# A two-layer graph kernel: the edge stage of each layer written out in source order, with its sums, node work and table writes cut into small steps

## The chip, the cores and the metric

The kernel runs on one core of a Trainium2 chip. The metric is the device time of one execution in microseconds (us). Engines are named as in the profile: PE (TensorE), DVE (VectorE), ACT (ScalarE), POOL (GpSimd) and SP (SyncE); PE, DVE, ACT and POOL compute, and SP, ACT and POOL also issue DMA transfers.

## What is computed

Two graph-transformer layers over 6250 nodes and 100,000 edges with 8 heads of 16 channels, then a linear layer, a residual and a layer norm. The edges are sorted by their target `dst`. Cut to what matters here:

```python
def gt_layer(x, ntype, etype, src, dst, Wk, Wq, Wv, Wa, Watt, Wmsg, pri, skip, g, b):
    k = typed_linear(x, ntype, Wk).reshape(n, H, HS)
    q = typed_linear(x, ntype, Wq).reshape(n, H, HS)
    v = typed_linear(x, ntype, Wv).reshape(n, H, HS)
    kT = jnp.einsum('nhd,htdo->nhto', k, Watt)
    vT = jnp.einsum('nhd,htdo->nhto', v, Wmsg)
    kw = kT[src, :, etype]
    m = vT[src, :, etype]
    a = jnp.einsum('ehd,ehd->eh', kw, q[dst]) * pri[:, etype].T / SQRT_D
    att = edge_softmax(a, dst, n)
    msg = (m * att[:, :, None]).reshape(-1, H * HS)
    hag = jax.ops.segment_sum(msg, dst, num_segments=n)
    h = jax.nn.silu(typed_linear(hag, ntype, Wa))
    alpha = jax.nn.sigmoid(skip[ntype])[:, None]
    h = h * alpha + x * (1.0 - alpha)
    ...
    return (h - mu) * jax.lax.rsqrt(var + 1e-05) * g + b
```

`typed_linear` uses one of 16 weight matrices for each node, by its type. So kT and vT together are a table with one row of 256 numbers for every pair of a node and one of 32 edge types, and each edge takes one row of it.

## The kernel before

**Tables.** For each layer the table is a DRAM tensor of 200,704 rows of 1 KB (`tabs`). The table of layer 0 is written first, from the inputs, beside the counting and ranking of nodes. The table of layer 1 is written by the node work of layer 0.

**Blocks.** The nodes are ranked into 52 blocks of 128, one node to a partition: 4 classes of 4 node types each, 13 blocks a class, by falling number of edges. A block has as many *slots* as its deepest node can have edges: 40, 23, 21, 19, 18, 17, 17, 16, 15, 14, 13, 12 and 11 in each class, 236 a class and 944 a layer. `superblocks` groups the 13 blocks of a class as 3, 3, 3 and 4, 16 superblocks in all.

**Edge work** (`edges`, from L737). For each slot POOL issues one indirect DMA (L754), which gathers 128 table rows, one for each partition, into a quarter of a `kv` tile. A `kv` tile holds a *chunk* of 4 slots (`CH`), and there are 12 of them. For each chunk DVE multiplies keys and query (L766) and adds up over the channels (L768). When a block's chunks are through, DVE adds the mask, takes the maximum and subtracts it (L773 to L778), ACT takes the exponential (L780), and DVE weighs the values of each chunk (L790), adds them into `acc` (L795) and reduces them (L796). Only L790 and L795 release a `kv` tile.

**Node work** (`nodes`, from L841). For each superblock: transpose on PE (L215), typed linear with `xm` masks on DVE (L200, PE L209), tanh on ACT (L856), residual (L865), norm statistics (L838, L839), reciprocal root by 13 small DVE instructions (`rstd_of`, L819 to L832), and norm (L872, L874). In layer 0 three typed linears follow, and then `table_block` (L220): for each block two halves of the edge types, each with 8 PE products of 32 rows (L229) and 8 ACT copies from PSUM into an `st` tile of 2 MB (L236), which POOL scatters into the table of layer 1 with one indirect DMA (L891). In layer 1 the last linear layer follows, and POOL scatters each block's output with one indirect DMA (L922). So POOL issues 944 gathers and 104 table scatters in layer 0, and 944 gathers and 52 output scatters in layer 1.

**What orders the work.** `edges` calls a generator `beside` once a chunk; it yields the queries of the next superblock and then the node work of the superblock before. This is the order in the source only. The program's scheduler, which works by priorities, is free to place the instructions of each engine otherwise, within the dependences; on each engine they then run in the order that it chose. The first gather of layer 1 depends on all table scatters (`puts`). Consecutive output scatters write the same tensor, and each waits for the one before to be complete; each POOL DMA also waits for the one eight places before it. PSUM pools: `qwp` 2 buffers, `accp` 2, `nps` 4, which the node work and `table_block` share under the name `nb`.

Of the kernel before, what the change touches and what calls it, by code (L numbers as in the profile page):

```python
# [9 lines left out]
F32 = mybir.dt.float32  # L10
# [3 lines left out]
ALU = mybir.AluOpType  # L14
# [55 lines left out]
def kernel(  # L70
# [91 lines left out]
    def load_edge_weights(l):  # L162
# [8 lines left out]

        nc.vector.tensor_scalar(prit, prit, 1.0 / float(HS) ** 0.5, None, op0=ALU.mult)
# [5 lines left out]
    load_edge_weights(0)  # L178
    load_typed(wq0, Wq[0])
# [38 lines left out]
    def table_block(pool, ps_pool, kT, vT, i, share, bufs, store):  # L218


        for tg in range(TG):
            tt = slice(tg * 16, (tg + 1) * 16)
            st = pool.tile([P, 16, 2 * D], F32, name="st", bufs=bufs)
            for half, (yT, bd) in enumerate(((kT, bdk), (vT, bdv))):
                for hp in range(HP):
                    s = slice(hp * 2 * HS, (hp + 1) * 2 * HS)
                    pt = ps_pool.tile([P, SB * P], F32, name="nb").rearrange(
# [450 lines left out]
    def arm(fast):  # L678

        puts = []  # L680
        ep = ctx2.enter_context(tc.tile_pool(name="ep", bufs=2))
        npl = ctx2.enter_context(tc.tile_pool(name="npl", bufs=1))
        qwp = ctx2.enter_context(tc.tile_pool(name="qwp", bufs=2, space=PSUM))
        accp = ctx2.enter_context(tc.tile_pool(name="accp", bufs=2, space=PSUM))
        nps = ctx2.enter_context(tc.tile_pool(name="nps", bufs=4, space=PSUM))
# [3 lines left out]
        if fast:  # L689
            for c in range(NC):  # L690
                for i0, k in superblocks(CB):
                    sbs.append((c * CB + i0, k, range(c * TC, (c + 1) * TC)))
        else:
            sbs = [(i0, k, range(TY)) for i0, k in superblocks(NB)]
# [9 lines left out]
        def old_rows(of, i0, k):  # L704
            hr = npl.tile([P, SB, D], F32, name="hr", bufs=3)
            nc.sync.dma_start(hr[:, :k], rows(of, i0, k))
            return hr

        def q_rows(ps, k):

            qT = npl.tile([P, SB * P], F32, name="qT")
# [3 lines left out]
            q = ep.tile([P, SB, D], F32, name="q")  # L715
# [3 lines left out]
        def queries0(got, i0, k, types):  # L719
# [6 lines left out]
            q = yield from q_rows(ps, k)  # L726
            got.append((q, ntb, hr))

        def queries1(got, i0, k, types):
            q = ep.tile([P, SB, D], F32, name="q")  # L730
            nc.sync.dma_start(q[:, :k], rows(qrd[1], i0, k))
            got.append((q, types_of(i0, k), old_rows(hrd, i0, k)))
            yield

        def edges(l, i0, k, q, beside):


            sums = ep.tile([P, SB, D], F32, name="sums")
            den = ep.tile([P, SB, H], F32, name="den")
            for i in range(k):  # L740
                b = i0 + i
                K = KB[b]
                qw = qwp.tile([P, 512], F32, name="qw")
                nc.scalar.copy(qw[:, :D], q[:, i, :])
                a = ep.tile([P, max(KB), H], F32, name="a")
                w = qw[:, D:D + K * H].rearrange("p (k h) -> p k h", h=H)
                chunks = [(j, min(j + CH, K)) for j in range(0, K, CH)]
                kvt = []
                for j0, j1 in chunks:
                    kv = ep.tile([P, CH, 2 * D], F32, name="kv", bufs=12)  # L750
                    kvt.append(kv)
                    for j in range(j0, j1):
                        at = KO[b] + j
                        get = nc.gpsimd.indirect_dma_start(  # L754
                            out=kv[:, j - j0, :], out_offset=None, in_=tabs[l][:],
                            in_offset=bass.IndirectOffsetOnAxis(ap=ell[:, at:at + 1], axis=0))
                        if l == 1:
                            for put in puts:
                                tc.add_manual_dep(
                                    get.ins, put.ins.name,  # L760
                                    mybir.DependencyInfo(mybir.DependencyClass.Sync,
                                                         mybir.DependencyReason.DATA),
                                    reason="rows of the table")
                            puts.clear()
# [33 lines left out]
            for _ in beside:  # L798
                pass
# [274 lines left out]
```

## Time and profile before

| | us |
|---|---|
| median of 3 runs (3934.1 to 3941.8) | 3939.6 |
| profiled execution, its own time | 3934.5 |
| its span in the trace | 3932.6 |
| first gather of layer 0's edge stage | at 918.3 |
| last gather of layer 0 | at 2420.3 |
| first gather of layer 1 | at 2589.1 |
| last gather of layer 1 done, about | at 3873.4 |
| DVE busy in the span | 2144.5 (55%) |
| POOL busy in the span | 2057.5 (52%) |
| PE busy in the span | 1969.3 (50%) |
| ACT busy in the span | 922.7 (23%) |

The page gives the busy time of each engine, the span in 40 slices, the costliest groups of instructions with the idle time ahead of them and what ended it. The trace can be asked for stretches of time, for waits by engine and for a timeline. `L754` is line 754 of the kernel before. `<-issue` after an idle time says that nothing which the profile shows ended it.

### The profile page before, as it was taken

The page shows a single profiled execution, that of the slowest core. Times are in us where ns is not written, and L with a number is a line of the kernel's source. Part 1 is how long each engine was busy: PE and PEld are TensorE (multiplying, and loading weights), DVE is VectorE, ACT ScalarE, POOL GpSimd, SP SyncE. Part 2 cuts the span into 40 slices and gives each one's busy share as a digit, 9 for nine tenths or more (in the row PEclk, how much of TensorE's full clock was granted, in tenths as well). Part 3 has the DMA queues.
Part 4 walks back from the last instruction along what each step waited for, and adds up shares of the span by engine and source line. Part 5 has one row for each costly group of instructions (what it writes and reads, how often), then busy time and mean ns, then how long its engine had stood idle before and what let it go on. Part 6 is the DMA issues. An engine that isn't in the chain of part 4 may idle for free. (4 is left out here: it accounts for less than half of the span.)

```text
span 3932.6 us, 25934 instructions
## 1 busy us (share of the span) xinstructions
PE 1969.3 (50%) x6850; PEld 1039.2 (26%) x6850; DVE 2144.5 (55%) x4929; ACT 922.7 (23%) x1928; POOL 2057.5 (52%) x2157
## 2 busy tenths in 40 slices
PE   2899967993165555666566657820221221122022
PEld 1345523331033333333234334410110110011011
DVE  6975632433655555455545554126655665665565
ACT  0244323451033232333233224420000000000000
POOL 0000072004766667656665664057776776777773
PEclk9999977995565566666666666755555555555555
DMA  4367548787366554675466558543343443333331
GB/s 89 160 264 310 239 132 324 324 339 248 104 215 218 199 205 162 244 262 207 146 241 259 199 176 306 204 159 115 110 113 95 115 112 102 109 111 107 105 103 51
DMA packets 216823, 716.14 MB, mean 182 GB/s; under 512 B 64437, under 2 KB 122670, under 8 KB 191615
## 3 DMA queue, kind: packets, MB, share of 16 engines
q0 software_dynamic: 110592, 459.50, 35.5%
q1 hardware_dynamic: 83425, 245.01, 16.2%
q10 hardware_dynamic: 22642, 9.82, 1.1%
q8 instruction: 58, 0.95, 0.1%
q14 instruction: 106, 0.87, 0.1%
HBM read 289.27 MB, written 438.40 MB: 185 GB/s over the span
## 5 line engine op out<-in xcount | busy, mean ns | idle before, releaser
L754 POOL DMA_INDIRECT kv<-tab,ell x1888 | 1795.4, 951 | 928.8 <-issue 504.4
L236 ACT COPY st<-nb 128x512 f32<-128x512 f32 x1420 | 738.3, 596 | 661.9 <-PE nb L229 428.0
L766 DVE TENSOR_TENSOR kv<-kv,qw 128x512 f32<-128x512 f32 (+3 forms) x512 | 326.7, 642 | 923.7 <-DMA kv<-tab,ell 890.7
L229 PE MATMUL nb<-bdv,kvT 32*128 32x512 f32 x832 | 385.3, 1042 | 144.9 <-ACT st L236 144.4
L229 PE MATMUL nb<-bdk,kvT 32*128 32x512 f32 x832 | 364.1, 1013 | 122.7 <-ACT st L236 122.7
L644 PE MATMUL l<-xm,wkqv 128*128 128x512 f32 (+1 forms) x832 | 395.4, 608 | 8.1 <-DVE xm L200 8.1
L215 PE MATMUL nb<-ident,hag 128*128 128x128 f32 x104 | 24.5, 366 | 597.2 <-DVE hag L809 597.2
L768 DVE TENSOR_REDUCE a<-kv 128x32 f32<-128x512 f32 (+3 forms) x512 | 320.6, 636 | 0.9
L566 POOL DMA_INDIRECT ell<-kvs,start x52 | 53.9, 1037 | 504.5 <-DVE gap L545 489.0
L200 DVE SCALAR_TENSOR_TENSOR xm<-ntb,nb 128x384 f32<-128x384 int32 (+1 forms) x256 | 133.2, 582 | 310.0 <-PE nb L215 310.0
L215 PE MATMUL nb<-ident,hs 128*128 128x128 f32 x104 | 32.6, 456 | 520.0 <-DVE hs L874 481.8
L891 POOL DMA_INDIRECT tab<-st,row x104 | 104.5, 1005 | 336.4 <-ACT st L236 322.3
L780 ACT ACTIVATE qw<-a 128x136 f32<-128x136 f32 (+11 forms) x104 | 30.7, 296 | 1002.7 <-DVE a L778 984.9
L795 DVE TENSOR_TENSOR acc<-kv,acc 128x512 f32<-128x512 f32 (+3 forms) x408 | 259.0, 635 | 0.2
L229 PEld LDWEIGHTS nb<-bdv,kvT 32*128 32x128 f32 x832 | 188.6, 282 | 266.0 <-ACT st L236 265.0
L234 DVE COPY st<-nb 128x512 f32<-128x512 f32 x196 | 135.1, 689 | 211.3 <-PE nb L229 113.4
L790 DVE TENSOR_TENSOR kv<-kv,qw 128x512 f32<-128x512 f32 (+3 forms) x408 | 247.4, 626 | 0.0
L229 PEld LDWEIGHTS nb<-bdk,kvT 32*128 32x128 f32 x832 | 173.5, 274 | 216.6 <-ACT st L236 207.0
L644 PEld LDWEIGHTS l<-xm,wkqv 128*128 128x128 f32 x832 | 149.4, 195 | 237.6 <-issue 207.2
L229 PE MATMUL nb<-bdv,yT 32*128 32x512 f32 x784 | 171.1, 695 | 65.5 <-ACT st L236 62.7
L200 DVE SCALAR_TENSOR_TENSOR xm<-ntb,hT 128x512 f32<-128x512 int32 (+1 forms) x208 | 133.9, 658 | 114.8 <-PE l L644 105.2
L209 PE MATMUL nb<-xm,wkqv 128*128 128x384 f32 (+1 forms) x384 | 173.7, 619 | 20.2 <-DVE xm L200 20.2
(197 smaller groups left out, 2339.9 us busy)
## 6 DMA issues: line engine op xcount, KB each, us to landing
tab<-st SPq DMA_DIRECT2D x98, 2048.0 KB, 7.1
kv<-tab,ell POOLq DMA_INDIRECT x1888
ntb<-typed SPq DMA_DIRECT2D x24, 192.0 KB, 3.2
xrd<-xr SPq DMA_DIRECT2D x13, 256.0 KB, 2.3
hr<-in_x_dram SPq DMA_DIRECT2D x10, 256.0 KB, 4.1
ntb<-in_node_type_dram SPq DMA_DIRECT2D x10, 256.0 KB, 6.7
hr<-xrd SPq DMA_DIRECT2D x12, 192.0 KB, 2.7
hrd<-hs SPq DMA_DIRECT2D x12, 192.0 KB, 2.4
```

Of the source, the lines that this page charges most:

```text
L200: nc.vector.scalar_tensor_tensor(xm[:, :n], ntb[:, :n], float(t), hT[:, :n], op0=ALU.is_equal, op1=ALU.mult)
L209: nc.tensor.matmul(ps[:, :n], w[:, t, :], xm[:, :n], start=(t == types[0]), stop=(t == types[-1]))
L229: nc.tensor.matmul(pt, yT[s, i * P:(i + 1) * P], bd[s, tt, :], start=True, stop=True)
L234: nc.vector.tensor_copy(to, pt)
L236: nc.scalar.copy(to, pt)
L644: nc.tensor.matmul(ps[i][:, :n], wkqv[:, i, t, :], xm[:, :n], start=(t == 0), stop=(t == TY - 1))
L754: get = nc.gpsimd.indirect_dma_start(out=kv[:, j - j0, :], out_offset=None, in_=tabs[l][:], in_offset=bass.IndirectOffsetOnAxis(ap=ell[:, ...
L766: nc.vector.tensor_tensor(kk, kk, qw[:, :D].unsqueeze(1).to_broadcast([P, j1 - j0, D]), op=ALU.mult)
L768: nc.vector.tensor_reduce(a[:, j0:j1, :], kk.rearrange("p k (h d) -> p k h d", h=H), axis=AX.X, op=ALU.add)
L790: nc.vector.tensor_tensor(to.rearrange("p k (h d) -> p k h d", h=H), v.rearrange("p k (h d) -> p k h d", h=H), w[:, j0:j1, :].unsqueeze(3) ...
L795: nc.vector.tensor_tensor(acc[:, :c], v, acc[:, :c], op=ALU.add)
L891: put = nc.gpsimd.indirect_dma_start(out=tabs[1].rearrange("(n t) c -> n (t c)", t=16), out_offset=bass.IndirectOffsetOnAxis(ap=row2[:, tg ...
```

## The change

- The arm of the program that runs here is recorded under `manual_schedule`: each engine takes its instructions in source order.
- The superblocks of a class are 4, 3, 3 and 3 blocks, with 103, 52, 45 and 36 slots (before: 84, 54, 48 and 50).
- `edges` now goes over a whole layer. The sums of a block (`finished`: mask, maximum, exponential, weighing and adding) are a generator, of which a step is taken after each product, each reduction and once more for each chunk of the *next* block: 3 steps a chunk. The first tile of a block is released in step 5.
- The node work has many more yields (34 steps are reckoned for layer 0 and 50 for layer 1) and is spread over the next superblock's slots.
- The table pieces of a superblock are a second list, spread over the slots of the superblock two further on (faster for the last four). A scatter is emitted three further steps after its tile was handed over, not at once. The last superblock's copies from PSUM are shared by ACT and DVE.
- The output scatters of a superblock are emitted together, 8 yields after the data; those of the last superblock at once.
- PSUM: `accp` 1 buffer, `nps` 2, and `table_block` has its own pool `tps` of 3. `hr` is loaded again for the node work. The scaling of layer 1's edge weights moves into the first node work.

No instruction of the edge work is added or removed: POOL still issues 1048 DMAs in layer 0 and 996 in layer 1. In the built program's POOL order, 13 table scatters follow the last gather of layer 0 (20 before), and the output scatters stand in 14 groups of 3 or 4 ahead of layer 1's last gather, with the last 6 behind it.

```diff
     def arm(fast):
...
-        accp = ctx2.enter_context(tc.tile_pool(name="accp", bufs=2, space=PSUM))
-        nps = ctx2.enter_context(tc.tile_pool(name="nps", bufs=4, space=PSUM))
+            accp = ctx2.enter_context(tc.tile_pool(name="accp", bufs=1, space=PSUM))
+        nps = ctx2.enter_context(tc.tile_pool(name="nps", bufs=2 if fast else 5, space=PSUM))
+        tps = ctx2.enter_context(tc.tile_pool(name="tps", bufs=3, space=PSUM))
...
-                    sbs.append((c * CB + i0, k, range(c * TC, (c + 1) * TC)))
+                    sbs.append((c * CB + CB - i0 - k, k, range(c * TC, (c + 1) * TC)))
+            sbs.sort(key=lambda sb: sb[0])
...
+            def spread(work, gen, steps, slots):
+
+                work.append([gen, steps / slots, 0.0])
+
+            def tick(n):
+                for of in (work, pieces):
+                    if of:
+                        w = of[0]
+                        w[2] += w[1] * n
+                        while w[2] >= 1.0:
+                            w[2] -= 1.0
+                            if next(w[0], of) is of:
+                                of.pop(0)
+                                break
...
+            def finished(s, i, chunks, kvt, a, w, sums, den):
...
+                yield
                 m = ep.tile([P, H], F32, name="m")
                 nc.vector.tensor_reduce(m, av.rearrange("p k h -> p h k"), axis=AX.X, op=ALU.max)
+                yield
                 nc.vector.tensor_tensor(av, av, m.unsqueeze(1).to_broadcast([P, K, H]),
                                         op=ALU.subtract)
                 nc.scalar.activation(w, av, AF.Exp)
-                next(beside, None)
+                yield
+                yield
                 nc.vector.tensor_reduce(den[:, i, :], w.rearrange("p k h -> p h k"),
                                         axis=AX.X, op=ALU.add)
                 acc = accp.tile([P, CH, D], F32, name="acc")
...
+                for j in range(len(chunks) + 1):
+                    if j < len(chunks):
+                        j0, j1 = chunks[j]
+                        v = kvt[j][:, :j1 - j0, D:]
+                        nc.vector.tensor_tensor(
...
+                    if j > 1:
+                        j0, j1 = chunks[j - 1]
+                        nc.vector.tensor_tensor(acc[:, :j1 - j0], kvt[j - 1][:, :j1 - j0, D:],
+                                                acc[:, :j1 - j0], op=ALU.add)
+                    yield
                 nc.vector.tensor_reduce(sums[:, i, :], acc.rearrange("p k c -> p c k"),
                                         axis=AX.X, op=ALU.add)
...
+                if i == k - 1:
+                    spread(work, nodes(l, *sbs[s], sums, den, got[s][1], lambda gen: table(s, gen)),
+                           50 if l else 34, pace(s + 1))
...
+                    tables[s] = gen
+                    spread(pieces, gen, 8 * sbs[s][1] + 4, (1.0 if s + 4 < len(sbs) else 0.6) * slots(min(s + 2, len(sbs) - 1)))
...
+                        nc.vector.tensor_tensor(
+                            kk, kk, qw[:, :D].unsqueeze(1).to_broadcast([P, c, D]), op=ALU.mult)
+                        step()
+                        tick(c / 3)
+                        nc.vector.tensor_reduce(a[:, j0:j1, :],
+                                                kk.rearrange("p k (h d) -> p k h d", h=H),
+                                                axis=AX.X, op=ALU.add)
+                        step()
+                        tick(c / 3)
+                        step()
+                        tick(c / 3)
...
+            while work or pieces:
+                for of in (work, pieces, pieces, pieces):
+                    if of and next(of[0][0], of) is of:
+                        of.pop(0)
...
+            for _ in range(8):
+                yield
+            for i in range(0 if final else k):
+                put_out(o, i0, i)
...
+            def steps(gen):
+
+                for _ in gen:
+                    for _ in range(2):
+                        for what in late:
+                            what[0] -= 1
+                        while late and late[0][0] <= 0:
+                            scatter(*late.pop(0)[1])
+                        yield
+
+            for i in range(k):
+                def store(tg, st, b=i0 + i):
+                    late.append([3, (tg, st, b)])
...
     with tc.If(full < 1) as cmp:
         with ExitStack() as ctx2:
+            ctx2.enter_context(tc.manual_schedule())
             arm(True)
```

## The prediction

> **What bounds the kernel now.** I read the page's busy shares first, then stretches of time by stage, then POOL's timeline and waits. No engine is busy over 55% of the span. The stretches below are the four classes of layer 0, the time between the layers, two classes of layer 1 and the end (columns: stretch, length, busy us and instruction count of PE, PE's weight loads, DVE, ACT and POOL, then clock, DMA share and GB/s):
>
> ```profile
> PE 1969.3 (50%) x6850; PEld 1039.2 (26%) x6850; DVE 2144.5 (55%) x4929; ACT 922.7 (23%) x1928; POOL 2057.5 (52%) x2157
> ```
>
> ```profile
> 918.30:1244.60 326.30, 120.84 (x298) 64.24 (x298) 179.15 (x390) 56.95 (x126) 231.57 (x244) 0.58 0.51 153
> 1244.60:1630.00 385.40, 233.75 (x617) 133.19 (x617) 204.87 (x482) 122.00 (x257) 249.96 (x262) 0.62 0.63 220
> 2025.10:2428.40 403.30, 247.75 (x679) 142.18 (x678) 214.30 (x505) 137.02 (x289) 251.90 (x263) 0.63 0.63 222
> 2428.40:2589.10 160.70, 133.01 (x377) 78.74 (x374) 28.79 (x96) 84.37 (x165) 18.66 (x20) 0.66 0.61 247
> 2895.30:3221.30 326.00, 62.20 (x149) 35.89 (x149) 201.57 (x549) 15.59 (x47) 237.37 (x249) 0.52 0.38 108
> 3873.40:3932.60 59.20, 17.14 (x44) 9.93 (x44) 27.68 (x96) 1.43 (x3) 6.92 (x7) 0.56 0.06 16
> ```
>
> POOL's timeline (start, length, idle before) gives the unit: a gather every 1.25 us, 0.95 of work and 0.30 that nothing ends. In layer 1, 249 x 1.25 = 311 of the 326 us. So POOL's issue is the bound there, and a full "busy" POOL shows 76%.
>
> ```profile
> 3609.65 0.95 POOL L754 DMA_INDIRECT kv<-tab,ell  x1 [0.30 <-issue]
> 3610.90 1.25 POOL L754 DMA_INDIRECT kv<-tab,ell  x1 [0.30 <-issue]
> 3619.38 0.94 POOL L754 DMA_INDIRECT kv<-tab,ell  x1 [7.23 <-DVE acc L790]
> 3620.63 0.94 POOL L754 DMA_INDIRECT kv<-tab,ell  x1 [0.30 <-issue]
> ```
>
> The 7.23 us recur once a class: the 40-slot block fills 10 of 12 kv tiles. Other stalls are table scatters that wait for ACT (POOL's waits from 1000 to 2400 us: total, times, longest), and output scatters that follow each other:
>
> ```profile
> POOL tab L891 <- ACT st L236: 178.5, 50, 8.4
> ```
>
> ```profile
> 3917.76 0.98 POOL L922 DMA_INDIRECT out_dram<-o,node  x1 [32.13 <-DVE o L920]
> 3920.76 0.98 POOL L922 DMA_INDIRECT out_dram<-o,node  x1 [2.02 <-issue]
> ```
>
> The ledger, in 1.25 us issues: start 918.3; layer 0, 1048 x 1.25 = 1310, and idle 1670.8 - 1310 = 361; layer 1 up to 3873.4, (944 + 45) x 1.25 = 1236, and idle 48; end 59. Sum 3932.6. Of the 361, the stretch from the last gather's end (2421.3) to layer 1's first (2589.1) holds 168 - 20 x 1.25 = 143, and the steady part 218.
>
> **What the Trainium skill says.** "PSUM — Partial Sum Buffer", section "Engine vs sequencer instructions": ACT, DVE and POOL queues are strict FIFO. So source order is run order, and one late operand holds all behind it; the stalls above agree. "DMA: Bandwidth & Descriptors", section "Anatomy of one DMA — SWDGE (gpsimd) path": a POOL DMA has about 2 us of fixed cost, mostly the receipt. The trace agrees: 2.02 us idle between chained output scatters, which start 3.00 us apart. "Perfetto Trace Analysis", section "Optimization Strategy": look at the gaps of the engine that should be full; a gap that repeats can mean too few buffers. That is the 7.23.
>
> **The change, part by part.**
>
> *POOL's issue work* is unchanged: 1310 in layer 0. In layer 1, 46 output scatters stand ahead of the last gather: 990 x 1.25 = 1237.5. The start (918.3) ends with the table of layer 0, which is not touched; the moved weight scaling is 0.42 + 1.22 us of DVE under POOL's first 48 gathers (60 us), and costs 1.6 us at most without that cover.
>
> *Sums as steps.* No DVE instruction goes. After the 40-slot block only two tiles are free, and its first is released in step 5 of the next block, in that block's second chunk. In layer 1: 1.5 us from issue to landing (from POOL's end to the transfer's semaphore, median of the trace), then product, reduction, sum and weighing (0.69 + 0.68 + 0.49 + 0.68) and a node row or two, about 5 us of stall; the next chunk's gathers take 5 us and its tile comes two DVE steps after landing, 4 us more. 9 us against 7.23, four times a layer: 36. Bounds 24 and 56.
>
> *Table scatters, layer 0 steady.* Before, six scatters came in a cluster one or two gathers apart, which is 3 us of POOL against 5.49 us a tile in ACT and PE (timeline of the tail: 2578.30, then 2583.79). Now they mostly have 4 or more gathers between them (6.25 us), and four half-steps after the last copy. So the rate stall goes. What is late next is position: POOL runs ahead of ACT, and ACT is tied to DVE and PE by exponentials and node work. Where a table tile is pressed into the 45 and 36 slots, the slack is about 5 slots, 7 us, against landing (2.4 on average in layer 0) and a half tile (2.7) with its copies (2.4): 7.5. DMA is at its limit there too: 0.79 x 5.49 = 4.3 us of all queues for a scatter, 4 x 0.39 x 1.25 = 2.0 for its gathers, 6.3 against 6.25. Every later gather queues behind a waiting scatter, and DVE waits for those. No row shows this wait. Bounds: 0, and 218/84 = 2.6 us a scatter as now. I take 0.9 for 91 scatters, 79 us. With 36 for the tile stalls: 115 (was 218).
>
> *Between the layers.* From the last gather's end (T): sums done T+12 (landing, last products, about 15 DVE rows). The tanh stands behind 32 copies in ACT's order, 4 x 5.49 = 22, so T+25. Tanh to key copies took 17.7 before (2458.66 to 2476.34), so T+43; to the first scatter 7.6, T+51; five more at 5.49, T+78; layer 1's gather 5.3 later (2583.79 to 2589.06), T+84. Less 13 x 1.25 = 16: 68, I take 70 (was 143: two chains one after the other). Bounds 62 and 95: the node chain alone takes 37 (2508.1 to 2545.3), or all 48 copies lie ahead of it.
>
> *Output scatters.* A chained one costs 3.00 - 1.25 = 1.75. 14 groups make 46 - 14 = 32 of them: 56. With 36 for tiles and 13 for scatters that wait for DVE in short superblocks (bounds 0 and 40): 105 (was 48). This part loses 57.
>
> *The end.* Before: 13.8 from the last gather to the transposes (3887.16), 30.6 to the first scatter, 3 x 3.0, 5.8 to the end. Now three scatters instead of four and three blocks (2.6 less a block in the last products, 1 to 2 of statistics out of the way): 52 (was 59).
>
> Reloading `hr` is 16 loads on SP's queue, 2.7 us each, behind nothing that gates a gather: nothing, or 3 us at each superblock's transposes if SP were late. PSUM with fewer buffers is inside the 0.9.
>
> Sum: 918.3 + 1310 + 115 + 70 + 1237.5 + 105 + 52 = 3808 span. The profiled execution's own time is 1.9 above its span, and the median 5 above that: **3815 us**, 3.2% less. Main case's own range 3765 to 3900.
>
> **The rivals.**
>
> *Clean*: no scatter waits. 36 + 62 + 92 + 50 in place of 115, 70, 105 and 52 is 102 less: 3713. For it: landing is 1.5 to 2.4 us. Against: the DMA count above.
>
> *The wait only moves*: each scatter still stalls 2.6 us: 91 x 2.6 + 36 = 273 of steady idle for 115, 158 more: 3973. For it: POOL in fixed order runs behind ACT as before. Against: the clusters are gone. No gain is left from 1.4 above my 0.9 a scatter (125 us).
>
> *Slower: DVE in fixed order pays the hand-overs.* Each superblock's node chain has some five places where DVE's next instruction needs PE or ACT. Bare, the tail shows 4.70 us for the tanh and 0.6 to 1.2 for each transpose, about 8 a superblock; behind a table half of 2.7 on PE each, up to 22. In the 45 and 36 slots POOL has (81 + 14) x 1.25 = 119 us. DVE has 0.75 us of edge work a slot (the four kv and acc rows of the groups, 1154 us in both layers, and 1.9 + 0.68 for each of 104 blocks: 1420/1888), 61, and 134/16 = 8.4 of node work and queries a superblock (834 busy in layer 0 less 944 x 0.75 = 708, some 130): 78, so 41 free. Waits of 2 x 8 fit, 2 x 22 just don't; it decides from 20 a superblock (4 a hand-over). If they reach 50, since PE itself waits for ACT's copies, 59 are over in each class, and kv tiles run out: 236 more, 4051. Against: DVE is 53% busy in layer 0, and free kv tiles let POOL run on. For it: the scheduler could place ready work there, source order can't.
>
> **How the numbers follow.** Main 0.58, clean 0.20, wait moves 0.12, hand-overs 0.10. A measurement of this kernel can tell about 0.2% from no change. Faster: main and clean less 0.02 for main's upper end: 0.76; same 0.04; slower, the last two less what falls between: 0.20. The range for 8 in 10 goes from the clean case (3715) to the moving wait (3975).
>
> **What would show it.** Right: POOL's 1.25 us cadence unchanged; layer 0's steady idle near 115, with scatter waits under 1 us on average; 13 scatters and near 70 idle between layers; chained output scatters 3.0 us apart, 32 of them, and a layer 1 slower than before by some 55; stalls of about 9 us after each 40-slot block. Wrong: kv waits of POOL that DVE's node chain ends, or a longer cadence for scatters (DMA), or layer 1 as fast as before.

## The result and the profile after

The changed kernel takes 4170.4 us (median of 4 runs, 4168.1 to 4170.9) where the kernel before takes 3940.7: a ratio of 1.058 with a 95% interval from 1.0565 to 1.060. It is slower by 230 us. The prediction was 3815, between 3715 and 3975.

The page of the changed kernel, busy time of each engine:

```profile
PE 2101.8 (50%) x6850; PEld 976.8 (23%) x6850; DVE 2202.5 (53%) x4953; ACT 919.6 (22%) x1904; POOL 2063.3 (49%) x2157
```

The engines run as many instructions as before, but for 24 copies that moved from ACT to DVE. PE is busy for 132 us more and DVE for 58; that alone doesn't make the kernel slow, since e4_scheduler below, with 2115 and 2177 us, runs the same instructions and is faster than the kernel before. POOL has the same 2157 instructions in a longer span. The granted clock of TensorE is 0.645 over the span, for 0.656 before and 0.661 in e4_scheduler; no run here separates it from the rest. The stretches of the changed kernel, in the columns that the prediction explained: two classes of layer 0, the time between the layers, one class of layer 1, the end.

```profile
922.60:1312.40 389.80, 176.16 (x403) 81.98 (x404) 191.90 (x422) 79.71 (x168) 238.61 (x249) 0.58 0.53 162
1312.40:1720.70 408.30, 262.02 (x628) 114.40 (x625) 215.81 (x502) 125.86 (x262) 250.28 (x261) 0.63 0.60 205
2574.30:2701.50 127.20, 110.57 (x269) 50.45 (x266) 40.25 (x94) 47.13 (x91) 12.84 (x15) 0.62 0.56 217
3031.90:3390.90 359.00, 57.20 (x149) 34.26 (x149) 208.59 (x551) 15.13 (x47) 238.00 (x250) 0.52 0.34 98
4106.90:4168.60 61.70, 20.86 (x56) 13.12 (x56) 28.60 (x109) 2.82 (x8) 6.10 (x6) 0.53 0.05 14
```

Read the POOL counts against the lengths: 261 instructions x 1.25 us are 326 of 408 us in a class of layer 0, and 250 x 1.25 = 312 of 359 in one of layer 1. What POOL waits for in layer 0 of the changed kernel up to the last gather (total, times, longest):

```profile
POOL tab L1068 <- ACT st L239: 205.0, 43, 23.0
POOL tab L1068 <- ACT qw L796: 66.3, 12, 13.5
POOL tab L1068 <- ACT qw L778: 54.4, 8, 13.5
```

These are table scatters that wait for a tile's copies. Where the profile names an exponential (L796) or a query copy (L778), that was ACT's latest instruction when POOL went on. POOL's timeline of the changed kernel in layer 1, the long gaps alone: two of three output scatters in a row, then the stall after a 40-slot block.

```profile
3049.43 1.01 POOL L1100 DMA_INDIRECT out_dram<-o,node  x1 [12.68 <-DVE o L1052]
3052.50 1.01 POOL L1100 DMA_INDIRECT out_dram<-o,node  x1 [2.06 <-DVE a L794]
...
3116.50 0.94 POOL L872 DMA_INDIRECT kv<-tab,ell  x1 [4.50 <-DVE acc L807]
3125.30 1.07 POOL L872 DMA_INDIRECT kv<-tab,ell  x1 [4.10 <-DVE hs L994]
```

The 7.23 us of before have become 4.50 + 4.10 (the first and the second tile of the next block); the gap that matters is new: 12.68 us at an output scatter whose rows DVE had not made yet.

The ledger of POOL, as in the prediction: start, idle time beside 1.25 us for each DMA in the steady part of layer 0, between the layers and in layer 1, and the end (positions of POOL's DMAs in each trace; us). The issue is 1310 and 1237.5, but 1236 in layer 1 of the three kernels with the superblocks in the order of before (before, g4_order, k2_best_order), which have one DMA less ahead of the last gather. In g1_late5 and k1_tail five scatters more fall between the layers than in the changed kernel.

| kernel | start | steady 0 | between | layer 1 | end | span |
|---|---|---|---|---|---|---|
| before | 918 | 218 | 143 | 48 | 59 | 3932.6 |
| predicted | 918 | 115 | 70 | 105 | 52 | 3808 |
| changed | 923 | 358 | 111 | 168 | 62 | 4168.6 |
| e4_scheduler | 918 | 127 | 107 | 48 | 52 | 3799.9 |
| e1_acc_sbuf_3 | 921 | 369 | 114 | 177 | 61 | 4188.8 |
| e2_acc_sbuf_4 | 920 | 308 | 83 | 177 | 61 | 4096.1 |
| e3_prefetch | 919 | 311 | 114 | 162 | 62 | 4115.2 |
| f1_outs | 919 | 356 | 114 | 45 | 62 | 4042.7 |
| f2_hand | 923 | 343 | 124 | 162 | 61 | 4160.8 |
| f3_fixed_all | 916 | 238 | 92 | 59 | 61 | 3914.1 |
| g1_late5 | 918 | 176 | 114 | 58 | 61 | 3875.0 |
| f4_sched_4 | 917 | 89 | 75 | 66 | 53 | 3746.9 |
| g3_best | 921 | 84 | 74 | 52 | 53 | 3730.7 |
| g2_qonce | 922 | 248 | 93 | 81 | 60 | 3950.4 |
| k1_tail | 916 | 173 | 107 | 59 | 61 | 3862.4 |
| g4_order | 922 | 75 | 109 | 58 | 56 | 3766.4 |
| k2_best_order | 916 | 55 | 83 | 73 | 56 | 3729.8 |

### The profile page after: what moved, and what is told of

It is laid out like the page before. It is cut to its first block, busy times and chain, and to the rows that moved or that the text cites. A ratio compares the mean times of both kernels' runs of the same rounds, so it can differ in the third digit from the quotient of the medians.

```text
span 4168.6 us, 25828 instructions
## 1 busy us (share of the span) xinstructions
PE 2101.8 (50%) x6850; PEld 976.8 (23%) x6850; DVE 2202.5 (53%) x4953; ACT 919.6 (22%) x1904; POOL 2063.3 (49%) x2157
## 5 line engine op out<-in xcount | busy, mean ns | idle before, releaser
L239 ACT COPY st<-tb 128x512 f32<-128x512 f32 x1396 | 744.9, 592 | 1019.8 <-PE tb L232 912.2
L884 DVE TENSOR_TENSOR kv<-kv,qw 128x512 f32<-128x512 f32 (+3 forms) x512 | 329.2, 643 | 1054.6 <-DMA kv<-tab,ell 956.0
L232 PE MATMUL tb<-bdk,kvT 32*128 32x512 f32 x832 | 429.6, 988 | 78.0 <-ACT st L239 77.9
L232 PE MATMUL tb<-bdv,kvT 32*128 32x512 f32 x832 | 413.1, 958 | 87.3 <-ACT st L239 87.0
L237 DVE COPY st<-tb 128x512 f32<-128x512 f32 x220 | 151.6, 689 | 250.7 <-PE tb L232 151.5
L218 PEld LDWEIGHTS nb<-ident,hag 128*128 128x128 f32 x104 | 17.7, 213 | 1017.4 <-issue 740.1
L807 DVE TENSOR_TENSOR kv<-kv,qw 128x512 f32<-128x512 f32 (+3 forms) x408 | 255.4, 626 | 0.0
L778 ACT COPY qw<-q 128x128 f32<-128x128 f32 x104 | 28.1, 271 | 807.5 <-DVE kv L807 806.9
L232 PE MATMUL tb<-bdv,yT 32*128 32x512 f32 x784 | 172.1, 693 | 66.7 <-ACT st L239 65.1
L232 PEld LDWEIGHTS tb<-bdv,kvT 32*128 32x128 f32 x832 | 144.0, 262 | 258.8 <-ACT st L239 231.7
L232 PEld LDWEIGHTS tb<-bdk,kvT 32*128 32x128 f32 x832 | 143.4, 265 | 245.0 <-ACT st L239 224.5
```

What stands on the lines that cost most here:

```text
L218: nc.tensor.transpose(tr[:, i * P:(i + 1) * P], src_of(i), ident)
L232: nc.tensor.matmul(pt, yT[s, i * P:(i + 1) * P], bd[s, tt, :], start=True, stop=True)
L237: nc.vector.tensor_copy(to, pt)
L239: nc.scalar.copy(to, pt)
L807: nc.vector.tensor_tensor((v if j else acc).rearrange("p k (h d) -> p k h d", h=H), v.rearrange("p k (h d) -> p k h d", h=H), w[:, j0:j1, ...
L884: nc.vector.tensor_tensor(kk, kk, qw[:, :D].unsqueeze(1).to_broadcast([P, c, D]), op=ALU.mult)
```

## The experiments

My theory after the result had three parts: the table's PSUM (three buffers for four), the loads of `hr` in SP's order, and output scatters placed ahead of their rows. The rival was that the written order as such costs the time, whatever these details.

**e4_scheduler: the same source, placed by the scheduler.**

```diff
-            ctx2.enter_context(tc.manual_schedule())
```

> The changed kernel's source, with the scheduler placing the usual arm's instructions instead of the source's order (one line taken out); everything else, the three PSUM buffers of the table too, as in the changed kernel. Theory FIFO: the written order is what costs, the time returns to near 3940 (3900 to 3980). Theory PSUM or SP: the structure costs, the time stays over 4060.

Measured: 3802.8 us, 0.966 of before (0.964 to 0.9675), so 368 us less than the changed kernel for one line. The whole loss, and more, lies in the order. The ledger says where: 231 us in the steady part, 120 in layer 1, 10 at the end, 4 between the layers and 4 at the start. POOL's waits in layer 0 under the scheduler, up to the last gather:

```profile
POOL tab L1068 <- ACT st L239: 108.3, 38, 12.0
```

Counted in POOL's order, the first 16 of the 104 table scatters stand up to 33 gathers later than in the changed kernel; from the 17th on each stands after the same number of gathers, but for one by four. The idle time at scatters in the steady part, beyond 0.3 us each, falls from 308 us to 104, and only 28 of these 204 are at the first 16. So for most of the loss POOL's own order isn't what was wrong; the copies come earlier, by the order on the engines that make them. The output scatters, though, stand 10 to 41 gathers later (first ones after gather 1124 of both layers for 1103), and most have gathers between them.

Which engine makes the copies late? The trace of the changed kernel can be followed back through each of the 50 longer stalls (0.6 us and more): from the scatter to the copy that released it, then to what that waited for or stood behind, as far as the start of the stall. Of their 314 us, PE's table products take 99, other products of PE (transposes and typed linears, which stand ahead of the table's in its order) 100, ACT's table copies 72, a late load of `hr` 15, and ACT's exponentials and query copies 5. In e4_scheduler the same count gives 47, 18, 35, 0 and 1 of 109. One such stall, from the changed kernel's timeline:

```profile
1181.11 0.90 PE L218 MATMUL nb<-ident,hag 128*128 128x128 f32 x3 [3.73 <-DVE hag L918]
1182.66 4.43 PE L212 MATMUL nb<-xm,wa 128*128 128x384 f32 x8 [0.65 <-DVE xm L203]
1187.02 1.13 PE L232 MATMUL tb<-bdv,kvT 32*128 32x512 f32 x6
1188.18 1.56 ACT L239 COPY st<-tb 128x512 f32<-128x512 f32 x3 [10.18 <-PE tb L232]
1190.84 1.02 POOL L1068 DMA_INDIRECT tab<-st,row  x1 [8.18 <-ACT qw L796]
```

PE stands at the node chain's transposes until DVE has made `hag`, then runs a typed linear of 4.43 us; the table's products come behind, then the copies, and POOL has stood for 8.18 us.

**e1_acc_sbuf_3 and e2_acc_sbuf_4: the table's PSUM.** The accumulator moves to SBUF, and then its bank to the table. To find the room, the rows `o` share a tile name with others here and in the runs below that need it.

```diff
-                acc = accp.tile([P, CH, D], F32, name="acc")
+                acc = ep.tile([P, CH, D], F32, name="acc", bufs=1)
...
-        tps = ctx2.enter_context(tc.tile_pool(name="tps", bufs=3, space=PSUM))
+        tps = ctx2.enter_context(tc.tile_pool(name="tps", bufs=4 if fast else 3, space=PSUM))
```

> Control for the next run: the sums' accumulator lies in SBUF instead of PSUM, the table's PSUM pool keeps 3 buffers. All theories: a table tile stays at 8 copies in groups of 3 (7.3 us), and the time stays within 0.7% of the changed kernel's 4170. If it drops by more than 1%, the one PSUM accumulator (products of a block waiting for the reduction of the block before) was itself a cause.

> The PSUM bank that the accumulator leaves goes to the table: 4 buffers. Theory PSUM (the table's products fell from four to three in a group, so a tile takes 7.3 us instead of 5.5): a tile is back at 5.5 us, the scatters' waits for ACT shrink, layer 0's idle of 358 us beside POOL's issues loses 100 to 200, the stretch between the layers 15 to 25; near 4010. Theory FIFO (POOL stands behind DVE's and ACT's order, whatever the tile's rate): the tile is 5.5 us and the time falls by under 40 us, 4130 to 4170. Theory SP (rows of x come late behind stores in SP's queue): under 40 us too.

Measured: 4190.9 and 4100.1, so the fourth buffer is worth 91 us: by the ledger 61 in the steady part and 32 between the layers. The theories of order and of SP's queue allowed less than 40; the near 4010 that I expected of the buffers is not reached. ACT's timeline of the changed kernel between the layers, and of e2_acc_sbuf_4 in the same place:

```profile
2632.31 1.56 ACT L239 COPY st<-tb 128x512 f32<-128x512 f32 x3 [1.18 <-PE tb L232]
2635.06 1.56 ACT L239 COPY st<-tb 128x512 f32<-128x512 f32 x3 [1.18 <-PE tb L232]
2637.80 1.56 ACT L239 COPY st<-tb 128x512 f32<-128x512 f32 x3 [1.18 <-PE tb L232]
```

```profile
2564.66 2.36 ACT L239 COPY st<-tb 128x512 f32<-128x512 f32 x4 [0.38 <-PE tb L232]
2567.40 2.37 ACT L239 COPY st<-tb 128x512 f32<-128x512 f32 x4 [0.38 <-PE tb L232]
```

A group takes 2.74 us either way, with as many copies in it as there are buffers. A tile is 8 copies: 8/3 x 2.74 = 7.3 us with three, 5.5 with four. The Trainium skill, "TensorE: Matmul & The Clock Gate", section "Part 3: Packing small matmuls — row/col tiling", says that products on different row groups of the array run beside each other, four of 32 rows 3.07 times as fast as in turn. The trace agrees with the beside (products of 1.2 us start 0.49 us apart), and no run here measures the factor. In this source each product has a PSUM buffer of its own, and as many finish in 2.74 us as there are buffers.

**e3_prefetch: the rows of x a superblock earlier.**

```diff
         def queries0(got, i0, k, types):
-            ntb, hr = types_of(i0, k), old_rows(xrd, i0, k)
+            if i0 not in loaded:
+                early(i0, k)
+            ntb, hr = loaded.pop(i0)
             hT = transposed(nps, lambda i: hr[:, i, :], k)
             yield
+            if fast and len(got) + 1 < len(sbs):
+                early(*sbs[len(got) + 1][:2])
```

> The rows of x and the types for a superblock's queries are loaded one superblock earlier, so no transposition can wait for them. Theory SP (PE waits 89 us in 13 places for these loads in layer 0, DVE and ACT behind it, the next block's query late): those waits go to zero and the time falls by 60 to 100 us, near 4085. Theories PSUM and FIFO: the waits go, the time falls by under 30 us, 4140 to 4170.

Measured: 4116.2, 54 us less. In the changed kernel, PE's wait in layer 0 for these rows, and the waits of SP's queue that stand ahead of such a load:

```profile
PE nb L218 <- DMA hr<-xrd: 89.4, 13, 22.7
```

```profile
SPq L1005 <- DVE hs L998: 1183.3, 14, 164.4
SPq L1036 <- ACT q L725: 293.5, 13, 34.7
```

SP stands at the stores of the node work (L1005, L1036) until DVE and ACT have made their rows, and the load that is next in the source stands behind. In e3_prefetch PE's wait for `hr` is gone from the list. I said 60 to 100; so some 35 of the 89 us had been covered by other waits.

**f1_outs: output scatters later and apart.** They go over the list of table pieces, which is empty in layer 1; `o` has two buffers.

```diff
-            for _ in range(8):
-                yield
-            for i in range(0 if final else k):
-                put_out(o, i0, i)
+            if not final:
+                table(put_outs(o, i0, k))
+
+        def put_outs(o, i0, k):
+            for i in range(k):
+                for _ in range(4 if i else 10):
+                    yield
+                put_out(o, i0, i)
```

> Output scatters of layer 1 are issued further behind the rows they send, and with at least four gathers between two of them (they go over the queue of table pieces, which is empty in layer 1; their tile has two buffers). Nothing else moves. Theory POSITION (the written place is what POOL pays for: scatters that come before DVE has made their rows, and chained ones): both waits go, layer 1's idle time falls from 168 to about 60, and the time to about 4060 (4045 to 4085). Rival DVE LATE (DVE itself lags, any place waits): only the chaining goes, 32 x 1.75 = 56, so 4115.

Measured: 4049.0, 121 less, all of it in layer 1 (168 to 45 in the ledger). An output scatter of f1_outs in POOL's timeline:

```profile
3060.52 0.95 POOL L872 DMA_INDIRECT kv<-tab,ell  x1 [0.30 <-issue]
3061.77 1.01 POOL L1104 DMA_INDIRECT out_dram<-o,node  x1 [0.30 <-issue]
3063.09 0.97 POOL L872 DMA_INDIRECT kv<-tab,ell  x1 [0.30 <-issue]
```

It fits between two gathers like a gather, where one in the changed kernel waited 12.68. The rival (DVE late wherever they are placed) falls. The two edits, later (by up to 67 gathers) and apart, aren't separated.

**f2_hand: empty steps at the hand-overs.** Two steps more in four places like this one, with 42 and 58 steps reckoned for 34 and 50.

```diff
             hT = transposed(nps, lambda i: hag[:, i, :], k)
             yield
+            for _ in range(2):
+                yield
```

> Two empty steps more behind each of the four places where the node chain's next DVE instruction needs PE or ACT (steps per superblock 42 and 58 for 34 and 50, so the chain takes the same number of slots). Theory HAND-OVER (DVE in fixed order stands at these places and POOL behind it): DVE's waits for PE's transposes (108 us) and for the tanh (77) in layer 0 fall by more than half, and the time falls by 50 to 100 us, to about 4095. Rival PLACE AND RATE (POOL waits for table copies and output rows; DVE's standing is hidden): DVE's waits shrink but the time stays within 25 us of 4170.

Measured: 4160.2, only 10 less, and the interval of its ratio to before (1.055 to 1.058) overlaps that of the changed kernel: not clear of no change. By the ledger 15 us go in the steady part and 6 in layer 1, and 13 come back between the layers. DVE's waits in layer 0 of the changed kernel, then of f2_hand:

```profile
DVE xm L203 <- PE nb L218: 107.8, 20, 21.2
DVE th L980 <- ACT th L973: 77.0, 15, 7.5
```

```profile
DVE xm L203 <- PE nb L218: 87.9, 10, 19.7
DVE th L984 <- ACT th L975: 13.4, 5, 4.3
```

The wait for the tanh, 5.1 us each time, is all but gone and the time hardly moves: most of it was covered. The wait for PE fell less than I expected, so this run doesn't price that one. e4_scheduler says more: DVE waits as long for PE in its layer 0, and that kernel is 368 us faster than the changed one.

```profile
DVE xm L203 <- PE nb L218: 113.0, 25, 21.4
```

**f3_fixed_all: these four at once, in the written order** (with more tiles sharing names to find the room in SBUF).

> All mends in the written order at once: four PSUM buffers for the table with the accumulator in SBUF, query rows loaded a superblock earlier, output scatters later and apart, empty steps at the hand-overs. If these four are what the written order costs beside the scheduler's, the gains add (90 + 54 + about 110 + up to 80 of 4170 to 4190): 3850 to 3930. If the order loses in many other places too, it stays over 3950.

Measured: 3916.7, 0.995 of before (0.993 to 0.9965). The parts add up: 4170 less 70 (e2_acc_sbuf_4 against the changed kernel), 54, 121 and 10 is 3915. So the buffers, the early rows and the places of the output scatters are causes side by side (the fourth part is not clear of no change), and the written order still loses 114 us to e4_scheduler, which has none of these mends.

**g1_late5 and h1_late5: scatters further behind the copies.**

```diff
-                    late.append([3, (tg, st, b)])
+                    late.append([5 if fast else 3, (tg, st, b)])
```

> The mended written order of f3_fixed_all (3917 us), with each table scatter issued five steps behind its tile's last copy in place of three. Theory SLACK (POOL's remaining waits of 161 us at scatters in layer 0 come from a place too near to the copies, which the scheduler hides by letting ACT run earlier): those waits fall by more than half and the time to about 3850. Rival BUFFERS (a later scatter holds one of three table tiles longer, and ACT's copies wait for it instead): within 25 us of 3917, or slower.

Measured: 3877.8, 39 less than f3_fixed_all. POOL's waits for copies in layer 0, f3_fixed_all and then g1_late5:

```profile
POOL tab L1087 <- ACT st L239: 121.3, 35, 11.4
POOL tab L1087 <- ACT qw L803: 41.4, 10, 9.1
POOL tab L1087 <- ACT qw L785: 20.6, 3, 10.2
```

```profile
POOL tab L1087 <- ACT st L239: 95.0, 37, 10.2
POOL tab L1087 <- ACT qw L803: 15.2, 4, 7.3
```

The steady part loses 61 us, but 22 come back between the layers, where 18 scatters follow the last gather for 13. The waits fall by almost two fifths, where I had said more than half: the slack is a cause in the mended kernel, at a price.

> The changed kernel with nothing but its table scatters issued five steps behind a tile's last copy in place of three. In the mended kernel this brought 39 us. Theory SLACK (the place of the scatters is a cause by itself): 40 to 80 us less than 4170. Rival RATE FIRST (with the tile at 7.3 us ACT is behind anyway, and the three tiles are held longer): within 20 us of 4170.

This run and the three below with h fell on another chip, where the kernel before took 4352 us and DVE stood up to 7 us at places where the trace names no cause; only ratios to before can be compared, and they don't carry over well: the kernel of h2_tail has 0.996 there and 0.983 on the first chip (k1_tail), that of h4_best_order 0.969 and 0.949 (k2_best_order). h1_late5 is 1.058 of before (1.054 to 1.062), as the changed kernel on its chip; a gain of 40 us, 1% of the time, could be hidden in that. So what the slack is worth without the faster tile stays untested.

**g2_qonce: one query copy for each superblock, exponentials in SBUF.**

```diff
-                qw = qwp.tile([P, 512], F32, name="qw")
-                nc.scalar.copy(qw[:, :D], got[s][0][:, i, :])
-                return qw
+                if i == 0:
+                    qw = qwp.tile([P, SB, D], F32, name="qw")
+                    nc.scalar.copy(qw[:, :sbs[s][1]], got[s][0][:, :sbs[s][1], :])
+                    whole.append(qw)
+                return whole[-1][:, i, :]
...
-                    w = qw[:, D:D + K * H].rearrange("p (k h) -> p k h", h=H)
+                    w = a[:, :K, :]
```

> f3_fixed_all, with the query rows of a superblock copied to PSUM in one ACT instruction instead of one for each block, and the exponentials written to SBUF in place. ACT then no longer stands at a block's query copy until DVE has read the buffer of two blocks before (254 us of ACT's waits in layer 0). Theory TIE (ACT in fixed order is tied to DVE there, the table's copies stand behind, and POOL's scatters behind those): ACT's wait goes, POOL's waits at scatters fall by half, time near 3850. Rival SLACK or BUFFERS: within 25 us of 3917.

Measured: 3954.9, 38 slower than f3_fixed_all. My expectation was wrong: ACT's waits in layer 0 of f3_fixed_all, then of g2_qonce:

```profile
ACT qw L785 <- DVE kv L814: 262.6, 31, 26.9
ACT qw L803 <- DVE a L801: 163.8, 28, 12.3
```

```profile
ACT a L807 <- DVE a L805: 373.3, 30, 37.2
```

The wait moved from the query copy to the exponential behind it: ACT still follows DVE. POOL's idle time at scatters in the steady part fell by 18 us, a tenth, where the theory asked for half. What made the kernel slower is elsewhere (see the last section). So this run, which left ACT's waits almost as long, doesn't test the tie.

**f4_sched_4, g3_best, g4_order, k2_best_order: the scheduler's order with the mends, and the order of the superblocks.** f4_sched_4 is e4_scheduler with the two edits of e2_acc_sbuf_4; g3_best adds those of e3_prefetch and f1_outs. g4_order is e4_scheduler with

```diff
-                    sbs.append((c * CB + CB - i0 - k, k, range(c * TC, (c + 1) * TC)))
+                    sbs.append((c * CB + i0, k, range(c * TC, (c + 1) * TC)))
```

and k2_best_order is g3_best with the same edit.

> The scheduler's order with the accumulator in SBUF and four PSUM buffers for the table, to beat both kernels. Theory RATE (the stretch between the layers, and a few dense superblocks, wait for the tile's 7.3 us): 20 to 50 us less than the scheduler's 3803, near 3765. Rival: the scheduler hides the rate, so 3795 to 3825.

> The scheduler's order with all mends that helped (four PSUM buffers, early query rows, output scatters apart): if the scheduler leaves anything to the latter two, 3720 to 3745; if it hides them already, 3750 to 3765.

> The changed kernel under the scheduler (3803 us) with the superblocks of a class in the order before (3, 3, 3 and 4 blocks). Tells how much of the structure's gain the order brings. Theory: with 36 slots in three blocks last in place of 48 slots in four the end and the tail between the layers are shorter by some 10 us each, and the short superblocks crowd the table more: 3795 to 3835. Rival: the table of the large superblock then falls on too few slots, over 3840.

> The best version so far (g3_best, 3732 us) with the superblocks in the order before. If its gain of 35 us under the scheduler adds to the mends: 3690 to 3710. If the four PSUM buffers have taken the crowding away already: 3720 to 3740.

> The kernel of h4_best_order again, likewise: g3_best (3732 us) with the superblocks in the order before. If the 35 us that this order brought under the scheduler add to the mends: 3690 to 3710. If the four PSUM buffers have taken that crowding away already: 3720 to 3740.

Measured: f4_sched_4 3755.2, g3_best 3731.7, g4_order 3767.7, k2_best_order 3733.5 (h4_best_order, on the other chip, 0.969 of before). So the two edits are worth 48 us under the scheduler as well: 38 in the steady part and 32 between the layers, less 18 that layer 1 loses, where POOL's issue gets longer with the accumulator in SBUF (last section). The new order of the superblocks costs 35 us, against my guess: 51 in the steady part (127 for 75 in g4_order), of which the other parts give some back. In g3_best and k2_best_order, with all mends, the two orders are level; but the order of before is still 28 us better in the steady part (55 for 84) and loses that in layer 1 (73 for 52), between the layers and at the end. These kernels differ from the first two in three mends, so which of them levels the orders isn't shown. g3_best is the best kernel found: 0.948 of before (0.946 to 0.9495).

**k1_tail (h2_tail on the other chip) and h3_order_written: what is left in the written order.** Both are edits to g1_late5; h3_order_written takes the order of the superblocks of before.

```diff
-                for of in (work, pieces, pieces, pieces):
+                for of in (work, pieces):
```

> g1_late5 (3878 us), with the last node chain of a layer taking turns with the table pieces one to one behind the last gather, where the source gives three pieces to each step of the chain. Theory TAIL (the chain stands behind copies in ACT's and PE's fixed order, and the last six tiles wait for it): the stretch between the layers, 47 us longer than the scheduler's, loses 20 to 40, time 3840 to 3860. Rival: the copies are what the stretch waits for, so it stays or grows, 3870 to 3900.

> The kernel of h2_tail again, on a chip where the kernel before takes near 3937 (on the chip of h2_tail it took 4352, and DVE stood 3 to 7 us at places that nothing in the trace explains). Theory TAIL (between the layers the node chain stands behind table copies in ACT's and PE's fixed order): the idle time of the last superblock of layer 0 falls from g1_late5's 136 us by 20 to 40, the time from 3878 to 3840 to 3860. Rival (the copies are what it waits for): 3870 to 3900.

> g1_late5 with the superblocks of a class in the order before (3, 3, 3 and 4 blocks). Under the scheduler this brought 35 us: in the short superblocks of 45 and 36 slots up to 15 table tiles and the node chain fall on too few gathers, and 84, 54, 50 and 48 slots spread them. Theory CROWDING (it holds in the written order too, more so, since a late copy stands in POOL's way): 40 to 80 us less, 3800 to 3840. Rival (the large superblock's table in the written order is the bound): within 20 us of 3878.

Measured: k1_tail 3868.7, 9 less than g1_late5, and 114 to 107 between the layers: the rival (the copies are what the stretch waits for) holds nearly. h2_tail and h3_order_written took 4330.5 and 4300.5 on the other chip. They differ in two edits, and g1_late5 was not run there, so what the order of the superblocks is worth in the written order isn't shown.

## Why the prediction was wrong

**The mechanism that decided.** I priced the written order at 0.9 us a table scatter and 13 us of output scatters that wait for DVE, and otherwise as if an instruction ran once its operands were there. I had quoted that one late operand holds all behind it, and applied it to POOL and, in part, to ACT; what stands behind PE's and SP's waits had no line in the sum. The change gives up the scheduler's placement, and that costs 368 us (e4_scheduler). Under the scheduler two terms of the sum hold: layer 0's steady part (127 against 115) and the end (52 against 52). That e4_scheduler's whole span, 3800, lies near my sum of 3808 is luck: it is 37 us longer between the layers and 57 shorter in layer 1. The loss by the steps of the prediction:

- *Issue*: right. POOL's cadence is 1.25 us before and after, 13 scatters are left after the last gather.
- *Sums as steps, 9 us a 40-slot block*: right, 4.50 + 4.10, four times in layer 1. (In the kernel before the 7.23 us came three times there, not once in each of the four classes.)
- *Table scatters, 0.9 us each, bounds 0 and 2.6*: this step failed most. The 91 scatters of the steady part waited 308 us beyond the 0.3 of issue, 3.4 each, above my upper bound, which I had taken from the kernel before as if the change could only keep or shorten that wait. In the written order, 61 us hang on the tile's rate, some 47 on the late rows of x, 61 on slack of two more steps (with the former mended, and 22 of it given back). Inside the stalls it is PE, more than ACT's exponentials, which I had named, that holds the copies up.
- *"PSUM with fewer buffers is inside the 0.9"*: wrong. It is 91 us, and it sets the time between the layers too: my 70 there used 5.49 us a tile. With four buffers that stretch is 75 (f4_sched_4) and 83 (e2_acc_sbuf_4); with three it was 111. The path was right and only its size off, since the rate it rests on had changed.
- *"Reloading `hr` ... nothing, or 3 us at each superblock's transposes if SP were late"*: I took nothing, and SP was late: PE waited 89 us in 13 places for the query rows of x, and loading them earlier gained 54. I counted the load's 2.7 us and not what SP's queue is standing at ahead of it. Whether the reload itself or the fixed place of the stores makes the queue late, no run separates.
- *Output scatters*: the 32 chained ones cost their 1.75 us each as said. The 13 us for scatters that wait for DVE (upper bound 40) were 66 (63 without their issue), from one row of POOL's waits in layer 1 of the changed kernel:

```profile
POOL out_dram L1100 <- DVE o L1052: 66.0, 10, 12.7
```

- *The end*: 62 for 52, which the scheduler's order does give.
- *The rivals*: my slower case, DVE's hand-overs in fixed order, had the right sign and the wrong place. It decides, I said, from 20 us a superblock; DVE's waits at the tanh and the transposes in layer 0 come to 12 (107.8 + 77.0 + 8 us over 16 superblocks), and f2_hand took the tanh's away for 10 us at most. (Its sum has a slip: 834 less 708 is 126, not 134; it moves the 41 us of room by less than one.) Nearer was "the wait only moves", whose price per scatter was too low by 0.8 us and which left out the output scatters.

**What stays open.** With the same buffers, early rows and places of the output scatters the scheduler's order is still 137 us faster than the best written order (g3_best 3732, k1_tail 3869, which has the slack besides): by the ledger 89 in the steady part, 33 between the layers, 8 at the end and 7 in layer 1, less 5 at the start. So the mends name only a part of what the order costs, and some of them help the scheduler's order too. ACT, in fixed order, stands at exponentials and query copies until DVE comes, with table copies behind them; but inside the stalls of the changed kernel this accounts for 5 of 314 us, and PE's other products for 100. What delayed the copies before a stall began isn't in this count, and no run moved the products of PE, so PE's part is read from the trace and not shown by an experiment.

## What to carry to other kernels

When a change takes an engine's order out of a scheduler's hands, make that a line of the sum of its own, and price it first: for each instruction that waits, list what is queued behind it on its engine, PE included, stores on SP's queue too, and on POOL everything. A scatter in fixed order wants to stand well behind the work that feeds it and apart from its like: most of the output scatters, 4 to 67 gathers later and with gathers between them, were worth 121 us here. And count PSUM buffers as a rate: here, one buffer fewer of four made each tile a third slower.

## What the runs showed of the hardware

With the accumulator in SBUF for PSUM, POOL's issue of a gather gets longer in the mean. The gather's row in the groups of the changed kernel, e1_acc_sbuf_3 (accumulator in SBUF) and g2_qonce (the weights too); columns: count, busy us, mean ns, idle before:

```profile
L872 POOL DMA_INDIRECT kv<-tab,ell x1888 | 1800.8, 954 | 938.3 <-issue 810.3
```

```profile
L871 POOL DMA_INDIRECT kv<-tab,ell x1888 | 1823.9, 966 | 937.5 <-issue 811.2 <-DVE acc L806 29.7 <-DVE acc L813 19.8
```

```profile
L883 POOL DMA_INDIRECT kv<-tab,ell x1888 | 1868.5, 990 | 950.5 <-issue 806.3 <-DVE acc L818 17.4 <-DVE t L953 14.6
```

On the first chip these busy times are 1795 to 1801 us in the seven kernels with the accumulator in PSUM, and 1824 to 1830 in the eight with it, but not the weights, in SBUF. The trace says where the difference lies: in the changed kernel 4 of the 475 gathers that run beside an addition into the accumulator take over 1.0 us, in e1_acc_sbuf_3 107 of 461. The 23 us are about what e1_acc_sbuf_3 loses to the changed kernel (20): the ledger has 11 more in the steady part, 3 between the layers and 9 in layer 1, while POOL's idle times in layer 0's steady part and layer 1 hardly move. g2_qonce has 43 us more than f3_fixed_all (1825.1) and is 38 slower, but there 18 us of scatter waits went as well and 5 came at the start. The Trainium skill, "SBUF — State Buffer", section "SBUF: two separate sides", says that DVE and GpSimd share a port pair, which the one that starts first holds for its whole instruction: a DVE instruction in a two-port mode, or, against a GpSimd operation that reads SBUF, one with two SBUF inputs. The addition has two SBUF inputs once its accumulator is there, so the direction agrees. Whether a gather's issue is such an operation, and whether it is the port that it waits for, no run here shows.
